# Last states of GpSimdE's quads copied by ScalarE, and half of the fifth quad to GpSimdE in every pass

## The chip, the cores and the metric

One core of a Trainium2 chip runs the whole program in one launch. The metric is the device time of an execution in microseconds. A kernel is timed in several runs and the median counts. One further execution is recorded by the hardware profiler: its trace gives the start and the length of every instruction on the engines TensorE (PE), VectorE (DVE), ScalarE (ACT), GpSimdE (POOL) and on the DMA queues, which SyncE (SP) mostly feeds.

## What is computed

The input is `x`, two images of 256 channels and 4096 positions. A state-space layer (a Mamba block with 256 inner channels) is added to it, then two more, one that runs forward over the positions and one that runs backward (512 inner channels each), then a mixture of 8 experts of three dense layers. The change touches only the recurrence of the three state-space layers, which is this, for every inner channel `d` and each of 16 states `s`:

```python
def step(h, inp):
    dt_t, B_t, C_t, x_t = inp
    h = h * exp(dt_t[..., None] * A) + (dt_t * x_t)[..., None] * B_t[:, None, :]
    y = einsum('bds,bs->bd', h, C_t)
    return (h, y)
```

So for each channel and state there is a decay `exp(dt * A)`, an input `dt * x * B`, a linear recurrence over 4096 positions, a product with `C`, and a sum over the 16 states.

## The kernel before

**Tiling.** Each layer of each image is a job (`Scan`); there are 6, with `nj` = 2, 4 and 4 blocks of 128 channels for each image. A job runs over 8 chunks of `T` = 512 positions. A chunk of a job is a step; a step has `nj / 2` passes; a pass treats two blocks of channels in 8 quads, `n` = 0 to 7. That makes 48 steps, 80 passes and 640 quads (`quads`, L665), numbered `g`. "Even" and "odd" passes below are those with `g // QN` even or odd, counted from 0. A quad is a tile of 128 rows by 4 groups of 512 positions. A row is one of 32 channels together with one of four states, so that a quad covers 128 channels and 4 of their 16 states.

**The work on a quad** comes from these small functions.
- `emit_b` (L738): GpSimdE multiplies the input by `B` into the quad's tile `bq` (L742, 128x2048). `bq` has six buffers.
- `emit_decay` (L744) and `emit_join` (L757): ScalarE makes the decays of half a quad (two groups) into a PSUM tile `da` with two `Exp` (L752). There is one `da` buffer for each half. Since one scan runs over two groups at once, the decay at the border is set so that nothing passes it, and the state of the second group is added to its first input by the small activation in `emit_join` (L763), which reads the state `h`.
- `emit_scan` (L773): VectorE scans half a quad, 128x1024 (L778). The first group's state is the scan's initial value. The result goes into `bq`, where GpSimdE is to take the product with `C`, else into `da`.
- The product with `C`: VectorE does it for half a quad in `emit_times_c` (L787, from `da` into `bq`), GpSimdE for a quad in `emit_times_c_quad` (L803, in place in `bq`; 128x2048, or 128x1024 for half a quad).
- The last state of each group is kept in `job.h` for the next chunk. ScalarE copies it from `da` in `emit_carry` (L797, two values in a row) where VectorE does the product. GpSimdE copies it from `bq` at the head of `emit_times_c_quad` (L802, four values in a row, two for half a quad) where GpSimdE does it.
- `emit_sum` (L808): TensorE sums the four states of a quad into `y` (L811); `emit_gate` (L822) is VectorE's.

**Who takes which product** is told by `on_pool` (L768): the quads 0, 2 and 5 of every pass (`POOL_C`) are GpSimdE's, and in odd passes also the first half of quad 4 (`POOL_HALF`).

**Order.** The main loop (L1105) goes over quads and halves; a half is a slot. In a slot, each engine's instructions are issued in the order of the text, and `in_order` (L158) ties every instruction to the one before it on its engine, so this is the order in which each engine runs. ScalarE has in a slot: the states of the slot before (`emit_carry`), the join and the decays of the slot after (`emit_decay`), then what the slots' plan puts there (`sl.run(slot, "act")`: activations of the projections, softplus, table loads, copies out of PSUM, the experts). VectorE has its scan, then gates and other planned work, then its product. GpSimdE has at the first half of each quad what `POOL_AT` (L66) says: `b` is an input product, three or more quads ahead, `c` a product with `C`, `h` that of the half:

```python
POOL_AT = {0: "b3", 1: "c0 b4", 2: "b5", 3: "c2 b6", 4: "b7", 5: "h4 b8", 6: "c5 b9", 7: "b10"}
```

After it follow the planned products `dt * x` (`xdt`, L598). TensorE's sums are placed by `SUMS` (L65): those of quads 2 and 3 at quad 4, that of quad 4 at quad 6, those of 5 and 6 at quad 7. TensorE runs the projections, convolutions and experts in between, in order, so a sum that waits holds up what follows. The plan of slots and expert work is made beforehand and doesn't depend on the lines that the change touches.

After the last quad a second stage computes the remaining experts and adds up (L1154 and after).

Of the kernel before, what the change touches and what calls it, by code (L numbers as in the profile page):

```python
# [50 lines left out]
T = 512  # L51
# [4 lines left out]
QN = 8  # L56
# [4 lines left out]
POOL_C = (0, 2, 5)  # L61

POOL_HALF = (4, 0)
# [73 lines left out]
def hybrid_kernel(ctx: ExitStack, tc: tile.TileContext, a: dict, out: bass.AP):  # L137
    nc = tc.nc
# [55 lines left out]
    with ExitStack() as st:  # L194
# [155 lines left out]
        steps = [(job, c) for job in jobs for c in range(NCH)]  # L350
# [318 lines left out]
        bq, da, y = {}, {}, {}  # L669
        pending, wanted = [], []  # L670

        def at(g):

            i, jp, n = quads[g]
            return i, 2 * jp + n // SG, n % SG
# [92 lines left out]
        def on_pool(g, h):  # L768

            n = quads[g][2]  # L770
            return n in POOL_C or (n, h) == POOL_HALF and g // QN % 2

        def emit_scan(g, h):  # L773
            i, j, sg = at(g)
            job, c = steps[i]
            d = da[g, h].rearrange("p q t -> p (q t)")
            b = bq[g][:, 2 * h : 2 * h + 2, :].rearrange("p q t -> p (q t)")
            nc.vector.tensor_tensor_scan(  # L778
                b if on_pool(g, h) else d, d, b,
                job.h[:, j, sg, 2 * h : 2 * h + 1] if c else 0.0, ALU.mult, ALU.add,  # L780
            )
# [10 lines left out]
        def emit_carry(g, h):  # L792

            i, j, sg = at(g)
            d, two = da.pop((g, h)), slice(2 * h, 2 * h + 2)
            if not on_pool(g, h):
                nc.scalar.copy(steps[i][0].h[:, j, sg, two], d[:, :, T - 1])  # L797

        def emit_times_c_quad(g, groups=SG):
            i, j, sg = at(g)  # L800
            b = bq[g][:, :groups, :]
            nc.gpsimd.tensor_copy(steps[i][0].h[:, j, sg, :groups], b[:, :, T - 1])  # L802
            nc.gpsimd.tensor_tensor(  # L803
                b, b,
                cks[i]["bc", 1, sg].rearrange("p (o t) -> p o t", o=1).to_broadcast([P, groups, T]), ALU.mult,
            )
# [298 lines left out]
        for g in range(nq):  # L1105
            i, jp, n = quads[g]
            for h in range(2):
# [14 lines left out]
                if slot:  # L1122
                    emit_carry(*divmod(slot - 1, 2))
# [9 lines left out]
                if not on_pool(g, h):  # L1133
                    emit_times_c(g, h)

                if h == 0:
                    for what in POOL_AT.get(n, "").split():
                        m = g - n + int(what[1:])
                        if what[0] == "c":
                            emit_times_c_quad(m)  # L1140
                        elif what[0] == "h":
                            if on_pool(m, 0):
                                emit_times_c_quad(m, SG // 2)
                        else:
                            want_b(m)
# [8 lines left out]
    with ExitStack() as st:  # L1154
# [5 lines left out]
        n, x, y, acc, wts, wb, lt, w_dram = {}, {}, {}, {}, {}, {}, {}, {}  # L1160
# [160 lines left out]
        def layer(x, l, e, tag):  # L1321
            h = mk.tile([P, KC, T], F32, tag=f"h{l}", name=f"h{l}_{tag}", bufs=2 + 2 * l)
            for m in range(KC):
                ps = psp.tile([P, T], F32, tag="ps", name=f"hp{l}_{tag}_{m}")
                for k in range(KC):
                    nc.tensor.matmul(  # L1326
                        ps, we[f"W{l + 1}", e][:, k, m * P : (m + 1) * P], x[:, k, :],
                        start=(k == 0), stop=(k == KC - 1),
                    )
                nc.scalar.activation(  # L1330
                    h[:, m, :], ps, AF.Relu,
                    bias=of[:, l, e, m : m + 1], scale=sc[:, l, e, m : m + 1],
                )
            return h
# [104 lines left out]
        for at, (b, i, e) in enumerate(pairs):  # L1439
# [5 lines left out]
            h = layer(n[b, i], 0, e, f"{i}_{e}_{b}")  # L1445
# [136 lines left out]
```

## Time and profile before

| what | value |
| --- | --- |
| median of 3 runs (lowest, highest) | 4978.65 us (4976.32, 4984.62) |
| the profiled execution, and its span | 4972.65 us, 4970.9 us |
| granted TensorE clock, mean | 0.933 |
| first and last scan (L778) start | 58.1 us, 4437.4 us |
| VectorE's scans | 1280, 2276 to 2346 ns each by form |
| VectorE's products with C | 760, of half a quad |
| GpSimdE's products with C | 240 of a quad, 40 of half a quad |
| ScalarE's decays (L752), joins (L763) | 2560 of 686 ns, 1120 of 384 ns |
| GpSimdE's `xdt` products (L598) | 160 of 1274 ns |

All of the recurrence lies between the first and the last scan; what comes later is the experts' stage. Busy time of an engine is the time in which one of its instructions is shown at work. An instruction's length is not quite what it takes of its engine, since the next may start a little before its end or after a gap; where it matters, starts are subtracted.

### The profile page before, as it was taken

The numbers are of one execution on the slowest core, as the hardware profiler recorded it, in microseconds if no ns is written. First come the engines' busy times: TensorE is split into PE (matmuls) and PEld (weight loads), VectorE is DVE, ScalarE is ACT, GpSimd is POOL, SyncE is SP. The second block draws the span as 40 slices with busy tenths as digits, with TensorE's granted clock in tenths as the row PEclk, the third lists the DMA queues.
The fourth block names the chain that finished last, engine by engine and source line by source line (L and its number), as shares of the span: only waits on it lengthen the run. The fifth ranks groups of instructions, "written<-read, shape, count | busy, mean of one in ns | idle before, by whom it ended". The sixth has DMA issues, their size and how long they took to land. (4 is left out here: it accounts for less than half of the span.)

```text
span 4970.9 us, 47346 instructions
## 1 busy us (share of the span) xinstructions
PE 4225.8 (85%) x14912; PEld 1476.1 (30%) x14912; DVE 4567.6 (92%) x3097; ACT 3613.1 (73%) x7304; POOL 4340.4 (87%) x1424
## 2 busy tenths in 40 slices
PE   5777777788776899989999899889868989999999
PEld 1222222222222233333333333333222333334444
DVE  6998999999999999999999999999999999975565
ACT  5777777777777788878788788888767888862232
POOL 6998999999999999999999999999999999960000
PEclk8778899989988999999999999999989999999999
DMA  5455454444444455446676555555534455536653
GB/s 193 158 184 171 154 171 158 158 145 155 164 157 148 173 183 177 165 174 237 241 246 222 170 173 170 189 169 190 175 121 153 165 187 176 186 131 233 226 168 127
DMA packets 335407, 875.26 MB, mean 176 GB/s; under 512 B 36314, under 2 KB 111860, under 8 KB 293172
## 3 DMA queue, kind: packets, MB, share of 16 engines
q1 hardware_dynamic: 326164, 835.39, 48.7%
q0 software_dynamic: 8992, 36.85, 2.9%
q8 instruction: 118, 1.93, 0.2%
q14 instruction: 133, 1.09, 0.1%
HBM read 673.27 MB, written 198.84 MB: 175 GB/s over the span
## 5 line engine op out<-in xcount | busy, mean ns | idle before, releaser
L742 POOL TENSOR_TENSOR bq<-rxdt,bc 128x2048 f32<-128x2048 f32 x640 | 2893.8, 4544 | 15.2 <-DMA rxdt<-xdtd 7.3
L752 ACT ACTIVATE da<-rdt,w_a 128x512 f32<-128x512 f32 x2560 | 1756.9, 686 | 70.0 <-DVE bq L778 23.6
L778 DVE TENSOR_TENSOR_SCAN da<-da,h_state,bq 128x1024 f32<-128x1024 f32 x664 | 1557.9, 2346 | 50.3 <-ACT da L752 34.7
L803 POOL TENSOR_TENSOR bq<-bq,bc 128x2048 f32<-128x2048 f32 (+1 forms) x280 | 1180.1, 4215 | 22.6
L778 DVE TENSOR_TENSOR_SCAN bq<-da,h_state,bq 128x1024 f32<-128x1024 f32 x456 | 1059.0, 2338 | 8.1 <-ACT da L752 7.9
L811 PE MATMUL y<-bq,stack 128*32 128x512 f32 x5120 | 742.2, 665 | 276.5 <-POOL bq L803 251.2
L787 DVE TENSOR_TENSOR bq<-da,bc 128x1024 f32<-128x1024 f32 x760 | 926.2, 1219 | 15.7
L992 PE MATMUL e<-eh,ew 128*128 128x512 f32 x1376 | 659.5, 613 | 43.3 <-DVE sp L594 14.4
L797 ACT COPY h_state<-da 128x2 f32<-128x2 f32 x759 | 119.0, 157 | 618.8 <-DVE bq L787 615.4
L763 ACT ACTIVATE bq<-h_state,bq,a 128x1 f32<-128x1 f32 x1120 | 430.0, 384 | 4.7 <-POOL bq L742 4.1
L811 PEld LDWEIGHTS y<-bq,stack 128*32 128x32 f32 x5120 | 140.6, 116 | 823.7 <-POOL bq L803 373.6
L458 PE MATMUL z<-nx,w_in 128*128 128x512 f32 x640 | 332.6, 650 | 59.3 <-DVE q L423 21.0
L992 PEld LDWEIGHTS e<-eh,ew 128*128 128x128 f32 x1376 | 247.7, 191 | 450.4 <-issue 240.5
L531 PE MATMUL conv<-xs,w_conv 64*64 64x512 f32 x2560 | 334.6, 603 | 22.7 <-ACT xs L515 20.4
L992 PE MATMUL e<-en,ew 128*128 128x512 f32 x688 | 324.8, 605 | 26.5 <-DVE xr L891 17.6
L458 PE MATMUL xs<-nx,w_in 128*128 128x512 f32 x640 | 318.9, 626 | 31.2 <-DVE sz L624 18.4
L1330 ACT ACTIVATE h<-hp,of,sc 128x512 f32<-128x512 f32 x168 | 130.6, 777 | 275.2 <-PE hp L1326 273.7
L843 PE MATMUL o<-sz,w_out 128*128 128x512 f32 x640 | 295.8, 601 | 0.0
L1005 ACT ACTIVATE eh<-e,of,sc 128x512 f32<-128x512 f32 x344 | 260.1, 768 | 47.3 <-PE e L992 46.9
L598 POOL TENSOR_TENSOR xdt<-sp,xc 128x512 f32<-128x512 f32 x160 | 203.2, 1274 | 43.6 <-DVE sp L594 43.6
L778 DVE TENSOR_TENSOR_SCAN da<-da,bq 128x1024 f32<-128x1024 f32 x96 | 219.4, 2285 | 2.6 <-issue 1.5
L458 PEld LDWEIGHTS z<-nx,w_in 128*128 128x128 f32 x640 | 125.1, 205 | 262.1 <-issue 147.8
(145 smaller groups left out, 4753.5 us busy)
## 6 DMA issues: line engine op xcount, KB each, us to landing
rxdt<-xdtd SPq DMA_DIRECT2D x160, 1024.0 KB, 6.0
rdt<-dtd SPq DMA_DIRECT2D x160, 1024.0 KB, 6.8
bc<-bcd SPq DMA_DIRECT2D x384, 256.0 KB, 3.2
ew<-in_W SPq DMA_DIRECT2D x172, 256.0 KB, 4.9
u<-u SPq DMA_DIRECT2D x86, 512.0 KB, 5.7
u<-eu SPq DMA_DIRECT2D x82, 512.0 KB, 4.4
dtd<-sp SPq DMA_DIRECT2D x160, 256.0 KB, 3.3
xdtd<-xdt SPq DMA_DIRECT2D x160, 256.0 KB, 3.4
```

The source lines that it names most:

```text
L458: nc.tensor.matmul(ps, job.matrices["in", half][:, k, j * P : (j + 1) * P], rhs, start=(k == 0), stop=(k == KC - 1),)
L531: nc.tensor.matmul(v[r][64 * col : 64 * col + 64, :], job.matrices["conv"][rows, 2 * jp + j, k, :], ck["xs", jp][rows, j, k : k + T] if k ...
L742: nc.gpsimd.tensor_tensor(bq[g], ck["rxdt", j], over_groups(ck["bc", 0, sg]), ALU.mult)
L752: nc.scalar.activation(da[g, h][:, k, :], cks[i]["rdt", j][:, q, :], AF.Exp, scale=steps[i][0].w["a"][:, j, q * SG + sg : q * SG + sg + 1],)
L763: nc.scalar.activation(bq[g][:, q, 0:1], job.h[:, j, sg, q : q + 1], AF.Identity, scale=cks[i]["a0", j][:, h, sg : sg + 1], bias=bq[g][:, ...
L778: nc.vector.tensor_tensor_scan(b if on_pool(g, h) else d, d, b, job.h[:, j, sg, 2 * h : 2 * h + 1] if c else 0.0, ALU.mult, ALU.add,)
L787: nc.vector.tensor_tensor(bq[g][:, two, :], d, cks[i]["bc", 1, sg].rearrange("p (o t) -> p o t", o=1).to_broadcast([P, 2, T]), ALU.mult,)
L803: nc.gpsimd.tensor_tensor(b, b, cks[i]["bc", 1, sg].rearrange("p (o t) -> p o t", o=1).to_broadcast([P, groups, T]), ALU.mult,)
L811: nc.tensor.matmul(y[i, j][q * CG : (q + 1) * CG, :], stack, bq[g][:, q, :], start=False, stop=(sg == SG - 1),)
L843: nc.tensor.matmul(v[m], job.w["out"][:, j, m * P : (m + 1) * P], ck["sz", j], start=False, stop=(j == job.nj - 1),)
L992: nc.tensor.matmul(ps, ew[l][:, k, m * P : (m + 1) * P], key[x][:, k, :], start=(k == 0), stop=(k == KC - 1),)
L1005: nc.scalar.activation(key[dst][:, m, :], key["ps", l, m], AF.Relu, bias=of[:, l, e, m : m + 1], scale=sc[:, l, e, m : m + 1],)
```

## The change

GpSimdE's copy of the last states leaves `emit_times_c_quad`. `emit_carry` makes it on ScalarE, from `bq`, once per quad, after the second half's scan: four values in a row. For the fifth quad (`n` = 4), where GpSimdE has the first half alone, ScalarE copies two values from `bq` after that half's scan, and two from `da` after the other half's, as before. `on_pool` no longer asks for an odd pass, so the first half of quad 4 is GpSimdE's in every pass: its scan writes `bq`, VectorE's product of that half goes in the even passes, and `emit_times_c_quad(m, SG // 2)` is issued there at quad 5.

```diff
         def on_pool(g, h):
 
             n = quads[g][2]
-            return n in POOL_C or (n, h) == POOL_HALF and g // QN % 2
+            return n in POOL_C or (n, h) == POOL_HALF
 
...
             d, two = da.pop((g, h)), slice(2 * h, 2 * h + 2)
             if not on_pool(g, h):
                 nc.scalar.copy(steps[i][0].h[:, j, sg, two], d[:, :, T - 1])
+            elif h or not on_pool(g, 1):
+                upto = 2 * h + 2
+                nc.scalar.copy(steps[i][0].h[:, j, sg, :upto], bq[g][:, :upto, T - 1])
 
         def emit_times_c_quad(g, groups=SG):
             i, j, sg = at(g)
             b = bq[g][:, :groups, :]
-            nc.gpsimd.tensor_copy(steps[i][0].h[:, j, sg, :groups], b[:, :, T - 1])
             nc.gpsimd.tensor_tensor(
                 b, b,
                 cks[i]["bc", 1, sg].rearrange("p (o t) -> p o t", o=1).to_broadcast([P, groups, T]), ALU.mult,
```

## The prediction

> **What bounds the kernel now.** I read the busy shares first, then the groups by line with shapes kept apart, the waits of GpSimdE, the busy time of stretches, and last the timeline of one pass.
>
> ```profile
> PE 4225.8 (85%) x14912; PEld 1476.1 (30%) x14912; DVE 4567.6 (92%) x3097; ACT 3613.1 (73%) x7304; POOL 4340.4 (87%) x1424
> DVE  6998999999999999999999999999999999975565
> POOL 6998999999999999999999999999999999960000
> ...
> L742 POOL TENSOR_TENSOR bq<-rxdt,bc 128x2048 f32<-128x2048 f32 x640 | 2893.8, 4544 | 15.2 <-DMA rxdt<-xdtd 7.3 <-issue 7.3 <-PE y L811 0.6
> L803 POOL TENSOR_TENSOR bq<-bq,bc 128x2048 f32<-128x2048 f32 x240 | 1086.1, 4525 | 19.4
> L803 POOL TENSOR_TENSOR bq<-bq,bc 128x1024 f32<-128x1024 f32 x40 | 94.0, 2349 | 3.2
> L802 POOL COPY h_state<-bq 128x4 f32<-128x4 f32 x240 | 49.8, 208 | 36.2 <-DVE bq L778 36.0
> L802 POOL COPY h_state<-bq 128x2 f32<-128x2 f32 x40 | 10.7, 268 | 0.0
> L787 DVE TENSOR_TENSOR bq<-da,bc 128x1024 f32<-128x1024 f32 x760 | 926.2, 1219 | 15.7
> L797 ACT COPY h_state<-da 128x2 f32<-128x2 f32 x759 | 119.0, 157 | 618.8 <-DVE bq L787 615.4 <-DVE kept L305 1.6
> ...
> 1525.00:2382.00 857.00, 760.25 (x2720) 267.58 (x2713) 840.92 (x530) 682.57 (x1398) 852.46 (x266) 0.96 0.52 181
> 2382.00:2711.00 329.00, 300.11 (x978) 108.69 (x977) 308.02 (x185) 267.51 (x551) 316.78 (x97) 0.96 0.70 238
> 2711.00:3365.00 654.00, 589.09 (x2155) 202.75 (x2154) 645.46 (x420) 534.09 (x1075) 648.70 (x211) 0.96 0.55 176
> 3581.00:4336.00 755.00, 642.10 (x2400) 218.02 (x2398) 742.64 (x482) 587.29 (x1207) 751.06 (x239) 0.94 0.46 163
> ...
> 1800.89 2.33 DVE L778 TENSOR_TENSOR_SCAN da<-da,h_state,bq 128x1024 f32<-128x1024 f32 x1
> 1802.15 1.28 ACT L660 ACT_TABLE_LOAD   x1
> 1803.44 0.39 ACT L763 ACTIVATE bq<-h_state,bq,a 128x1 f32<-128x1 f32 x1
> 1802.98 0.19 POOL L802 COPY h_state<-bq 128x4 f32<-128x4 f32 x1
> 1803.25 4.53 POOL L803 TENSOR_TENSOR bq<-bq,bc 128x2048 f32<-128x2048 f32 x1
> 1835.61 2.36 POOL L803 TENSOR_TENSOR bq<-bq,bc 128x1024 f32<-128x1024 f32 x1
> 1837.92 4.57 POOL L742 TENSOR_TENSOR bq<-rxdt,bc 128x2048 f32<-128x2048 f32 x1
> ```
>
> The shares hide two stages: until about 4440 us VectorE and GpSimdE are both full; then the experts' tail runs on TensorE and GpSimdE is empty. The change touches the first stage alone; I take the tail as shifted, not changed. In the stretches (busy PE, PEld, DVE, ACT, POOL after the length) GpSimdE fills 99.5% of 1525 to 2382 (passes 26 to 41) and of 3581 to 4336 (passes 64 to 77), and no wait of it is listed there: it sets the pace. Elsewhere it sometimes waits for a scan, in front of its copy of states (L802): 36.0 us in 29 places, of which 6.5 in 176 to 402, 6.4 in 402 to 526, 5.0 in 526 to 1305, 4.3 in 1305 to 1525, 9.3 in 2382 to 2711, 1.8 in 2711 to 3365, 1.9 in 3365 to 3581. There VectorE, or ScalarE behind it, sets the pace.
>
> **What the Trainium skill says.** "Perfetto Trace Analysis", Optimization Strategy: the most-contended engine can change from regime to regime, and each is read by its own gaps. The trace agrees: two regimes inside one stage. "GPSIMD Engine Reference", 3.1 Elementwise: a two-input fp32 product of 2048 takes 4497 ns there, twice VectorE's. The rows say 4525 and 4544, and 2349 for half. "SBUF — State Buffer", Who interferes with whom: a VectorE instruction with at most one SBUF input, outside the two-port modes, doesn't contend with GpSimdE. Scans and products here read da from PSUM and one SBUF tile, and the L742 durations have 4543 for median and 4504 for minimum, so I stretch nothing. "Perfetto Trace Analysis", Optimizing Scalar/DVE Operations: ScalarE's access overhead is about 93 ns on SBUF, 51 on PSUM, and a profiled latency about twice that. L797 (from PSUM) shows 157 ns and the small SBUF copies L514 and L517 183 and 197; they agree.
>
> **The change by parts**, per pair of passes (one even, one odd; 40 pairs).
> GpSimdE's copies go. From L802's start to L803's is 0.27 us (1802.98 to 1803.25), duration and gap; 7 per pair: -1.89. (Busy 60.5 and the 22.6 idle ahead of L803 give 0.297 on the mean; the excess is a dozen long copies next to a DMA issue, which I don't count as gained.)
> The half product in even passes is added: 1835.61 to 1837.92, +2.31. Sum for GpSimdE +0.42 per pair, +16.8 in all; with 0.297, +0.23 and +9.3.
> VectorE loses one L787 in each even pass. Next start after one is 1.13 us later (1821.97 to 1823.10), and a scan followed by its product takes 2.38 (1815.36 to 1817.74) where one followed by another scan takes 2.24: -1.27 per pair, -51 in all. The scan itself only changes where it writes (2346 against 2338 ns): nothing.
> ScalarE gains 7 copies per pair. No row shows this form; from below the 0.04 by which L763 follows L797 (1806.97 to 1807.01), from above the full 0.20 of L517. I take 0.10, half of it, as the skill's page has it: +0.7 per pair, 28 in all (11 to 56). Queued behind each are the join (L763) and the two decays of the next slot, which VectorE's next but one scan needs. The decays already waited for that same scan to free da, so nothing new blocks them but the copy and, behind it, the join: 0.20 + 0.39 + 1.40 from the end of the scan, against 2.24 + 1.13 until VectorE wants them (a product quad follows each of quads 0 and 2). Hidden, except where ScalarE is already late: VectorE's waits for da are 3.5 us in 402 to 526 and 14.8 in 2382 to 2711. Four pairs of 0.7: +2.8. In even passes the copy of quad 4's first half no longer stands behind an L787: a small gain, counted as nothing.
> GpSimdE's product overwrites bq, so it now waits for ScalarE's copy. Behind it stand the next products, and TensorE's sums wait for those. In pass 31 the scan ends at 1803.22, ScalarE comes out of its table load at 1803.43, the copy could be done at 1803.63; GpSimdE got there at 1802.98. Read so, pass by pass, it would be late in 60 places by 61 us in all: about 0.7 us at quad 0 of the odd passes of 26 to 41 and 64 to 77, 2.5 in those of 49 to 63. I take it as nothing, for this reason: GpSimdE's lag behind VectorE at quad 0 is now uneven (4.5 us in even, 2.0 in odd passes, as in 30 and 31), because the half is taken in odd passes alone. After the change, even passes cost GpSimdE 2.31 - 0.81 more and VectorE 1.27 less, so it comes 2.8 us later, relative to VectorE, to quad 0 of the odd pass: behind the copy, not ahead of it.
>
> **The sum by stretch.** Each gets +0.42 per pair less the waits listed, but no better than VectorE's -1.27 per pair. 1525 to 2382, 8 pairs: +3.4. 3581 to 4336, 7: +2.9. 2711 to 3365, 6: 2.5 - 1.8 = +0.7. 526 to 1305, 7: 2.9 - 5.0 = -2.1. 3365 to 3581, 2: 0.8 - 1.9 = -1.1. At the floor: 176 to 402, 2: -2.5; 402 to 526, 1: -1.3; 1305 to 1525, 2: -2.5; 2382 to 2711, 3: -3.8. The first and last pair: 0. Together -6.3, with ScalarE's 2.8: -3.5. The profiled execution took 4972.65 (span 4970.9), so 4969; the three runs have their median 6.0 higher, at 4978.65, and there the same change makes 4975.
>
> **Rivals.**
> A, a wash (this sum): 4975, own range 4964 to 4986.
> B, VectorE's relief arrives. For: VectorE is at 98% too, and in 526 to 1305 and 2711 to 3581 the two share the pace; GpSimdE's gaps there include 0.08 us ahead of each L803, and dense lag may keep it from ever waiting. Against: 99.5% in 30 passes can't shrink. If the 24 pairs outside these 15 (less the last) get 1.27 each, -30, plus 6.3, and no ScalarE cost: 4955. With the mean copy (0.297) a little more.
> C, slower: GpSimdE waits for ScalarE's copy. Place: quad 0 of odd passes, behind the table load. It decides if the lag there stays under 2.7 us, because TensorE, held by GpSimdE's sums, holds ScalarE and so VectorE as well. Price 0.7 x 15 + 2.5 x 7 = 28 on 6.3, less the 13 gained at the floors and in 526 to 1305: +21, 5000.
> D, ScalarE is the bound: all 28 us on the path, with the +6.3 and nothing gained: 5013. Against: ScalarE is 80% busy where GpSimdE rules, and waits 615 us at L797.
>
> **How the numbers follow.** A measurement of this kernel tells 0.2% (10 us) from no change. Chances: A 0.45, B 0.32, C 0.19, D 0.04. A splits 0.11 faster, 0.32 same, 0.02 slower; B 0.28 and 0.04 same; C 0.02 same, 0.17 slower; D slower. So faster 0.39, same 0.38, slower 0.23. The range reaches from B with the full gain to C: 4948 to 5002; A alone 4964 to 4986.
>
> **What would show it.** Right: L802 gone, 80 half products, 720 L787, about 1040 copies of ScalarE; GpSimdE's busy time near 4374 (4340 + 94 - 60) and idle under 40 until 4430; VectorE's waits longer in passes 26 to 41. C shows as GpSimdE waiting for ScalarE's copy at L803, over 10 us in sum. B shows as stretches of 526 to 1305 and 2711 to 3581 shorter by over 1 us per pair. Wrong in any case if passes 26 to 41 get shorter: then GpSimdE did not set the pace there.

## The result, and the profile after

The changed kernel takes 5011.09 us (median of 4 runs, 5006.35 to 5015.03), beside 4977.62 for the kernel before (4 runs, 4976.32 to 4984.62). The ratio is 1.0065, with a 95% interval of 1.0053 to 1.0077: slower, by some 33 us, where 4975 had been forecast. The profiled execution took 5006.35 us, its span is 5004.6, and the mean granted clock is 0.93 (0.933 before), so the clock explains nothing.

First the busy shares and the tenths of VectorE and GpSimdE, of the changed kernel:

```profile
PE 4216.6 (84%) x14912; PEld 1471.6 (29%) x14912; DVE 4539.7 (91%) x3057; ACT 3642.1 (73%) x7584; POOL 4381.3 (88%) x1184
DVE  6998999999999999999999999999999999974565
POOL 6898999999999999999999999999999999961000
```

At this grain only single tenths differ, two of GpSimdE's and one of VectorE's. The groups by line, shapes kept apart, show that the work moved as the diff says:

```profile
L742 POOL TENSOR_TENSOR bq<-rxdt,bc 128x2048 f32<-128x2048 f32 x640 | 2983.9, 4786 | 13.3 <-DMA rxdt<-xdtd 7.3 <-PE y L813 5.9
L805 POOL TENSOR_TENSOR bq<-bq,bc 128x2048 f32<-128x2048 f32 x240 | 1143.9, 4766 | 46.2 <-ACT h_state L800 42.5 <-PE gm L337 1.6 <-POOL bq L742 1.3
L787 DVE TENSOR_TENSOR bq<-da,bc 128x1024 f32<-128x1024 f32 x720 | 877.6, 1219 | 14.5
L805 POOL TENSOR_TENSOR bq<-bq,bc 128x1024 f32<-128x1024 f32 x80 | 208.7, 2609 | 12.9 <-ACT h_state L800 12.9
```

L805 is the product with C in place (L803 before), L800 ScalarE's new copy. There are 80 half products and 720 of VectorE's, and no copy is left on GpSimdE. Two things stand out. L805 now waits for ScalarE's copy. And GpSimdE's products seem to have become longer, 4786 ns where 4544 stood before; this is a matter of how a length is recorded. From one start to the next a full product takes 4.49 us on the mean in both kernels. The long records, of over 4.8 us, nearly all lie in passes 8 to 23 and 44 to 63, and the median spacing behind them is 4.49 us too. The Trainium skill says so as well ("Perfetto Trace Analysis", GPSIMD Engine Instruction: time them by the spacing of starts). All lengths of GpSimdE's work below are spacings of starts.

The waits of the changed kernel (total, times, longest one):

```profile
ACT h_state L797 <- DVE bq L787: 529.1, 436, 23.5
...
DVE da L778 <- ACT da L752: 70.5, 80, 4.5
...
POOL bq L805 <- ACT h_state L800: 55.3, 32, 11.8
```

Before, GpSimdE waited 36.0 us for VectorE's scans in front of its copy; now 55.3 for ScalarE in front of its product. VectorE's waits for decays have doubled from 35.7. One wait of ScalarE alone has 23.5 us.

A total doesn't tell which of these count. For that I cut both traces at the first scan of passes, the same points of the work in each, and compare the lengths (us; worked out from the starts of the scans):

```
passes            before   after   longer   as forecast
0-1                118.0   133.9    +15.9        0.0
2-7                349.7   351.4     +1.7       -3.1
8-21               779.1   778.3     -0.8       -2.1
22-25              220.3   217.3     -3.0       -2.5
26-41              856.8   867.4    +10.6       +3.4
42-47              328.6   325.9     -2.7       -1.7
48-59              654.6   654.5     -0.1       +0.7
60-63              215.3   220.1     +4.8       -1.1
64-77              755.2   763.8     +8.6       +2.9
78-79              104.1   104.2     +0.1        0.0
before, behind     589.2   587.8     -1.4        0.0
```

So the loss lies in two kinds of places: 15.9 us in the first pair of passes, where nothing had been forecast, and 24.0 in passes 26 to 41 and 60 to 77, where 5.2 had been. Passes 2 to 7 lie 4.8 us above the forecast; the rest is within 1.4 us of it.

**The first pair.** The timeline of VectorE, GpSimdE and ScalarE in pass 1 of the changed kernel (start, length, engine, and in brackets the idle time ahead and what ended it):

```profile
130.59 0.67 DVE L594 SCALAR_TENSOR_TENSOR sp<-dt,sp 128x512 f32<-128x512 f32 x1
131.18 22.08 DVE L920 TENSOR_TENSOR sc<-sc,bn 128x32 f32<-128x32 f32 x1
153.18 0.18 DVE L921 TENSOR_TENSOR of<-bn 128x32 f32<-128x32 f32 x1
...
128.38 9.03 POOL L742 TENSOR_TENSOR bq<-rxdt,bc 128x2048 f32<-128x2048 f32 x2
137.36 2.49 POOL L598 TENSOR_TENSOR xdt<-sp,xc 128x512 f32<-128x512 f32 x2
139.80 4.50 POOL L805 TENSOR_TENSOR bq<-bq,bc 128x2048 f32<-128x2048 f32 x1
144.25 8.95 POOL L742 TENSOR_TENSOR bq<-rxdt,bc 128x2048 f32<-128x2048 f32 x2
165.03 2.35 POOL L805 TENSOR_TENSOR bq<-bq,bc 128x1024 f32<-128x1024 f32 x1 [11.82 <-ACT h_state L800]
...
158.56 0.16 ACT L797 COPY h_state<-da 128x2 f32<-128x2 f32 x1 [23.45 <-DVE bq L787]
```

And the same place in the kernel before (L918 to L921 there are L920 to L923 after):

```profile
131.90 0.26 DVE L918 TENSOR_TENSOR sc<-sc,bn 128x32 f32<-128x32 f32 x1
132.08 4.56 DVE L919 TENSOR_TENSOR of<-bn 128x32 f32<-128x32 f32 x1
136.68 1.19 DVE L920 TENSOR_TENSOR of<-of,sc 128x32 f32<-128x32 f32 x1
137.90 1.19 DVE L921 TENSOR_TENSOR of<-of,bn 128x32 f32<-128x32 f32 x1
...
127.57 9.03 POOL L742 TENSOR_TENSOR bq<-rxdt,bc 128x2048 f32<-128x2048 f32 x2
136.55 2.49 POOL L598 TENSOR_TENSOR xdt<-sp,xc 128x512 f32<-128x512 f32 x2
138.98 0.19 POOL L802 COPY h_state<-bq 128x4 f32<-128x4 f32 x1
```

`shift()` (inside `scales`) is four small operations of VectorE on 128x32, once in the whole program. Each of them reads two operands in SBUF (the second one two parts of the same tile), as GpSimdE's products do. In the kernel before, the second of them already took 4.56 us, until GpSimdE went from its second product to `xdt` at 136.55, and the last two 1.19 each, one `xdt` product each. After the change the first takes 22.08 us: through seven instructions of GpSimdE, back to back, until the last ends, at 153.2, and GpSimdE has nothing to start. It has nothing because VectorE stands: no scan, so no copy of the state (11.82 us of waiting), and ScalarE stands for 23.45. The four operations now take VectorE from 131.18 to 153.73, 22.6 us, where they took from 131.90 to 139.01, 7.1. The difference, 15.4, is nearly all of the 15.9 that this pair loses.

**Passes 26 to 77.** Pass 31 of the changed kernel, the same moment as in the timeline that the prediction shows:

```profile
1807.13 1.92 PE L813 MATMUL y<-bq,stack 128*32 128x512 f32 x16 [2.25 <-POOL bq L805]
1815.44 3.60 PE L845 MATMUL o<-sz,w_out 128*128 128x512 f32 x8
...
1819.07 0.59 ACT L860 COPY xr<-o 128x512 f32<-128x512 f32 x1 [2.23 <-PE o L845]
1819.67 1.28 ACT L660 ACT_TABLE_LOAD   x1
1820.97 0.20 ACT L800 COPY h_state<-bq 128x4 f32<-128x4 f32 x1
1821.07 0.38 ACT L763 ACTIVATE bq<-h_state,bq,a 128x1 f32<-128x1 f32 x1
1821.24 4.53 POOL L805 TENSOR_TENSOR bq<-bq,bc 128x2048 f32<-128x2048 f32 x1 [0.70 <-ACT h_state L800]
...
1822.79 2.36 DVE L778 TENSOR_TENSOR_SCAN da<-da,h_state,bq 128x1024 f32<-128x1024 f32 x1 [0.87 <-ACT da L752]
```

This is case C of the prediction. The scan that made the state was over at 1816.29, but on ScalarE a copy out of PSUM comes first, which waits 2.23 us for TensorE, then a table load; only then the copy of the state. TensorE in turn had waited 2.25 us for GpSimdE's product of the pass before, until 1807.13, and from there it had no gap up to the product L845 that ScalarE's copy waits for: what GpSimdE waits for hangs on its own earlier work. GpSimdE loses 0.70 us, and behind the same pile VectorE's next scan is 0.87 late for its decays. The busy time in these stretches (length; busy PE, PEld, DVE, ACT, POOL) agrees:

```profile
1538.74:2406.12 867.38, 761.73 (x2722) 265.81 (x2715) 832.30 (x523) 688.43 (x1454) 862.35 (x218) 0.95 0.51 179
3606.59:4370.39 763.80, 641.25 (x2397) 215.83 (x2396) 735.48 (x476) 593.29 (x1255) 759.64 (x198) 0.94 0.46 161
```

GpSimdE is idle for 5.03 us of the first and 4.16 of the second, all ahead of L805. The rest is more work: from GpSimdE's first instruction of pass 26 to its first of pass 42, waits taken off, a pair of passes takes it 107.18 us where it took 106.64 (+0.54), and in passes 64 to 77 108.42 where it took 107.85 (+0.57). In passes 60 to 63 it is 108.86 for 107.96 (+0.90), and its waits there grew from 1.93 to 3.94 us. The forecast had +0.42.

### The profile page after: what moved, and what is told of

Read it like the earlier page. It is cut to its first block, busy times and chain, and to the rows that moved or that the text cites. A ratio compares the mean times of both kernels' runs of the same rounds, so it can differ in the third digit from the quotient of the medians.

```text
span 5004.6 us, 47517 instructions
## 1 busy us (share of the span) xinstructions
PE 4216.6 (84%) x14912; PEld 1471.6 (29%) x14912; DVE 4539.7 (91%) x3057; ACT 3642.1 (73%) x7584; POOL 4381.3 (88%) x1184
## 3 DMA queue, kind: packets, MB, share of 16 engines
q8 instruction: 118, 1.93, 0.2%
## 5 line engine op out<-in xcount | busy, mean ns | idle before, releaser
L742 POOL TENSOR_TENSOR bq<-rxdt,bc 128x2048 f32<-128x2048 f32 x640 | 2983.9, 4786 | 13.3 <-DMA rxdt<-xdtd 7.3
L778 DVE TENSOR_TENSOR_SCAN da<-da,h_state,bq 128x1024 f32<-128x1024 f32 x630 | 1478.5, 2347 | 83.4 <-ACT da L752 67.5
L805 POOL TENSOR_TENSOR bq<-bq,bc 128x2048 f32<-128x2048 f32 (+1 forms) x320 | 1352.6, 4227 | 59.0 <-ACT h_state L800 55.3
L778 DVE TENSOR_TENSOR_SCAN bq<-da,h_state,bq 128x1024 f32<-128x1024 f32 x490 | 1139.1, 2339 | 13.6 <-ACT da L752 13.6
L787 DVE TENSOR_TENSOR bq<-da,bc 128x1024 f32<-128x1024 f32 x720 | 877.6, 1219 | 14.5
L797 ACT COPY h_state<-da 128x2 f32<-128x2 f32 x719 | 112.5, 157 | 532.7 <-DVE bq L787 529.1
L458 PE MATMUL z<-nx,w_in 128*128 128x512 f32 x640 | 320.1, 629 | 63.8 <-ACT nx L493 24.7
L845 PE MATMUL o<-sz,w_out 128*128 128x512 f32 x640 | 298.9, 606 | 0.0
L598 POOL TENSOR_TENSOR xdt<-sp,xc 128x512 f32<-128x512 f32 x160 | 231.6, 1462 | 40.7 <-DVE sp L594 40.7
L778 DVE TENSOR_TENSOR_SCAN da<-da,bq 128x1024 f32<-128x1024 f32 x90 | 205.7, 2285 | 5.1 <-ACT da L752 3.0
```

What stands on the lines that cost most here:

```text
L458: nc.tensor.matmul(ps, job.matrices["in", half][:, k, j * P : (j + 1) * P], rhs, start=(k == 0), stop=(k == KC - 1),)
L742: nc.gpsimd.tensor_tensor(bq[g], ck["rxdt", j], over_groups(ck["bc", 0, sg]), ALU.mult)
L778: nc.vector.tensor_tensor_scan(b if on_pool(g, h) else d, d, b, job.h[:, j, sg, 2 * h : 2 * h + 1] if c else 0.0, ALU.mult, ALU.add,)
L787: nc.vector.tensor_tensor(bq[g][:, two, :], d, cks[i]["bc", 1, sg].rearrange("p (o t) -> p o t", o=1).to_broadcast([P, 2, T]), ALU.mult,)
L805: nc.gpsimd.tensor_tensor(b, b, cks[i]["bc", 1, sg].rearrange("p (o t) -> p o t", o=1).to_broadcast([P, groups, T]), ALU.mult,)
L845: nc.tensor.matmul(v[m], job.w["out"][:, j, m * P : (m + 1) * P], ck["sz", j], start=False, stop=(j == job.nj - 1),)
```

## The experiments

The expectations name their theories by letters. W: GpSimdE's product waits for ScalarE's copy behind the table load. L: no wait matters, GpSimdE just has more to do. S: the stall of VectorE at `shift()` is a loss by itself, apart from the other two. Other letters are spelt out where they stand. Ratios are against runs of the kernel before made together with each set; its medians there were 4978.31 us in the first set (E1 to E4), 4977.46 in the second (P1, P2, H1, H2) and 4977.13 in the third (E5, E6).

### E1: the copies alone

ScalarE copies, but the half product stays in odd passes. Against the changed kernel:

```diff
-            return n in POOL_C or (n, h) == POOL_HALF
+            return n in POOL_C or (n, h) == POOL_HALF and g // QN % 2
```

> Only the first part of the change: ScalarE copies the states, GpSimdE has the half of quad 4 in odd passes alone, as before. Theory W (GpSimdE's product waits for ScalarE's copy, and ScalarE is held by TensorE, which GpSimdE's sums hold): the copies save GpSimdE 1.9 us per pair, of which the waits at quad 0 of the odd passes take back 0.7 to 2.5; with the one long stall of VectorE in pass 1 (about 16 us) the time is within 10 us of before, 4970 to 4990. Theory L (only GpSimdE's load counts): 15 pairs at -1.9, VectorE then setting the pace: 4955 to 4965, and 16 more if the stall stays. Theory H (the added half is harmless, the copies alone cost): as slow as the changed kernel, 5005 to 5015.

Measured: 4995.41 us, ratio 1.0031 (1.002 to 1.0042). GpSimdE has less work than in the kernel before, and the program is slower than that one. L is out, at least alone; H, by which the copies alone cost as much as the whole change, is out as well; and the total is 5 us above what W had. First, VectorE's stall is here too, and the first pair is 12.7 us longer than before, most of the 17 that this kernel loses:

```profile
130.96 19.76 DVE L920 TENSOR_TENSOR sc<-sc,bn 128x32 f32<-128x32 f32 x1
```

Second, in passes 26 to 41 GpSimdE's work per pair falls from 106.64 to 104.90 us, 13.9 in eight pairs, and the stretch is as long as before (857.8 against 856.8). GpSimdE's waits in that stretch, in one row:

```profile
POOL bq L805 <- ACT h_state L800: 15.6, 8, 4.0
```

15.6 us, once in each odd pass: the whole saving is spent in front of ScalarE's copy. So W's wait takes any time that GpSimdE saves, unless the lag grows.

### E2: the half product alone

The kernel before, with the half product in every pass and the copies left on GpSimdE:

```diff
-            return n in POOL_C or (n, h) == POOL_HALF and g // QN % 2
+            return n in POOL_C or (n, h) == POOL_HALF
```

> Only the second part: GpSimdE keeps its copies and takes the half of quad 4 in every pass. Theory L: +2.6 us per pair where GpSimdE sets the pace (15 pairs, +39) and +1 to +2 in the 14 pairs where the pace is shared: 5025 to 5045. Theory W says the same here, since no copy of ScalarE is waited for, and no stall of 16 us in pass 1, because the gap between copy and product is still there. Theory H: about 4980.

Measured: 5052.96 us, ratio 1.014 (1.0125 to 1.0156), above the range expected. GpSimdE waits for nothing in passes 26 to 41 and takes 109.19 us per pair, +2.55; the prediction's prices make 2.31 + 0.27 = 2.58 for this edit. In passes 64 to 77 it is +2.58. So GpSimdE does set the pace there, the price of the half product was right, and of the two edits this is the costly one. Passes 8 to 21 and 48 to 59 lost 13.1 and 10.0 us, 1.8 per pair, as the expectation had it for a shared pace. What goes beyond its range is spread: passes 26 to 41 and 64 to 77 lost 44.2 us where it had 39, passes 60 to 63 lost 6.6, and some 9 came in the first and last pair and outside of the recurrence. The mean granted clock of this run was 0.922; what of these 9 goes to that stays open. At `shift()` there was no long stall:

```profile
131.16 2.92 DVE L918 TENSOR_TENSOR sc<-sc,bn 128x32 f32<-128x32 f32 x1
134.00 4.54 DVE L919 TENSOR_TENSOR of<-bn 128x32 f32<-128x32 f32 x1
```

VectorE got in where GpSimdE went from one product to the next, at about 134.0, and again at its next change, at 138.5. No copy ran at either of them, so the gap behind a copy, by which the expectation explains it, isn't directly what let VectorE in. The stall thus belongs to the copies' move, not to the half product.

### E3: `shift()` on GpSimdE

The changed kernel, with the four small operations issued on GpSimdE, at the same slot:

```diff
-                nc.vector.tensor_tensor(sc, sc, bn[:, :, M_G], ALU.mult)
+                nc.gpsimd.tensor_tensor(sc, sc, bn[:, :, M_G], ALU.mult)
...
-            sl.put(s0 - 11, "dve", shift)
+            sl.put(s0 - 11, "pool", shift)
```

(The other three operations likewise.)

> The changed kernel with the four small operations of L920 to L923 on GpSimdE's queue instead of VectorE's. Theory S (a VectorE instruction with two SBUF inputs gets no turn while GpSimdE's reading instructions follow one another without a gap; L920 took 22.1 us in the changed kernel): pass 1 is shorter by about 16 us, the whole 4992 to 4998. If L920's length is a mark of something else that stops VectorE there, no change: 5005 to 5015.

Measured: 4992.85 us, ratio 1.0027 (1.0016 to 1.0037). The first pair goes from 133.9 to 110.2 us; L920 takes 0.255 us on GpSimdE. That is 23.7 us less than in the changed kernel, and 7.8 less than in the kernel before, which paid for its own stall. The stretches of passes 26 to 41 and 60 to 77 stay within 1.1 us of the changed kernel's. The whole gains 18 by the medians, less than the pair alone: in the profiled execution passes 42 to 47 are 3.6 us longer than after and what lies outside the recurrence 8.4; the latter differs by as much between the executions profiled here. So S is shown, as a cause of its own.

### E4: the state's copy first

The changed kernel, with ScalarE's copy for GpSimdE's quads moved up: right after the scan that it reads, ahead of what the plan puts on ScalarE in that slot (the copy out of PSUM and the table load among it). For slots of these quads:

```diff
-                if slot:
+                if slot and not on_pool(*divmod(slot - 1, 2)):
                     emit_carry(*divmod(slot - 1, 2))
                 emit_decay(*divmod(slot + 1, 2))
-                sl.run(slot, "act")
+                if not on_pool(g, h):
+                    sl.run(slot, "act")
...
                 emit_scan(g, h)
+                if on_pool(g, h):
+                    emit_carry(g, h)
+                    sl.run(slot, "act")
```

> The changed kernel, with ScalarE's copy of a GpSimdE quad put ahead of the planned ScalarE work of its slot, so that it no longer stands behind a copy out of PSUM that waits for TensorE, nor behind a table load. Theory W: GpSimdE's waits for the copy (55.3 us in 32 places, 11.8 of it in pass 1) fall under 20, passes 26 to 41 and 64 to 77 lose 0.7 us per pair: 4995 to 5003. Theory L: the waits were cover for other lateness, and the time stays at 5005 to 5015. Against both: planned ScalarE work comes up to 1 us later in every GpSimdE slot; if that decides, slower than 5015.

Measured: 5009.42 us, ratio 1.0059 (1.0047 to 1.0072): the total missed its range. By stretch it did what W says: passes 26 to 41 are 5.4 us shorter than after, 60 to 63 5.0, 64 to 77 5.0, and GpSimdE's waits there have all but gone. But now every planned work of ScalarE in such a slot waits for a scan, in all passes. VectorE, which waits for that work:

```profile
DVE xc L544 <- ACT thx L540: 60.4, 53, 11.9
```

In the changed kernel this wait came to 35.2 us in 20 places. Passes 22 to 25 lost 6.3, 2 to 7 3.5, and 7 came from the end of the program, which varies by so much between executions. The fix was too broad, so E5 narrows it.

### E5: the copy first at quad 0 of odd passes only

As E4, where `slot % 16 == 1` in an odd pass (the second half of quad 0), and nowhere else. The copy's old place in the next slot is left out there.

```diff
-                if slot:
-                    emit_carry(*divmod(slot - 1, 2))
+                if slot % 16 != 2 or g // QN % 2 == 0:
+                    if slot:
+                        emit_carry(*divmod(slot - 1, 2))
                 emit_decay(*divmod(slot + 1, 2))
-                sl.run(slot, "act")
+                first = slot % 16 == 1 and g // QN % 2
+                if not first:
+                    sl.run(slot, "act")
...
                 emit_scan(g, h)
+                if first:
+                    emit_carry(g, h)
+                    sl.run(slot, "act")
```

> The changed kernel, with ScalarE's copy put ahead of its planned work at one place only: quad 0 of the odd passes, where the earlier trial lost nothing and won 5.4 us in passes 26 to 41, 5.0 in 60 to 63 and 5.0 in 64 to 77. Theory W: these gains without the losses of the earlier trial, 13 to 16 us: 4995 to 4999. If the gain there was bought by the other 240 places, no change: 5008 to 5014.

Measured: 4997.53 us, ratio 1.0035 (1.0023 to 1.0046), as expected. Passes 26 to 41 are 5.0 us shorter than after, 60 to 63 2.9, 64 to 77 4.9. Pass 31 again:

```profile
1817.68 0.18 ACT L800 COPY h_state<-bq 128x4 f32<-128x4 f32 x1
1819.97 0.59 ACT L860 COPY xr<-o 128x512 f32<-128x512 f32 x1 [2.11 <-PE o L845]
1820.58 1.28 ACT L660 ACT_TABLE_LOAD   x1
...
1821.27 4.67 POOL L805 TENSOR_TENSOR bq<-bq,bc 128x2048 f32<-128x2048 f32 x1
```

The copy is done at 1817.86, GpSimdE comes to its product 3.4 us later and doesn't wait. ScalarE's wait for TensorE and its table load are where they were; they just stand behind the copy now. In passes 26 to 41 GpSimdE's time per pair is 107.36 with its waits, where the changed kernel has 107.81: what remains over 106.64 is the load (0.50) and 0.22 of waits.

### E6: both repairs

E5 with E3's `shift()` on GpSimdE.

> The same, with L920 to L923 on GpSimdE's queue. If the two causes are apart and are all there is: 5011 less 14 less 18: 4976 to 4983, the time before. If there is a third one: over 4985.

Measured: 4971.47 us, ratio 0.9989 (0.9982 to 0.9995), below the range expected: this had 18 us for `shift()`, and the first pair alone gives 24.0. With the two causes repaired the time is that of the kernel before. But this kernel is also rid of the stall that the kernel before has of its own; beside that kernel without its stall (H1 below, 4968.31) it is 3.2 us longer. GpSimdE's larger load is still there: against the kernel before, passes 26 to 41 are 6.5 us longer, 60 to 63 2.2 and 64 to 77 3.4.

### P1 and P2: what a small operation of VectorE waits for

The stall came with the copies' move, though no copy runs during it. To see whether it happens elsewhere, both kernels got `shift()` on GpSimdE and 12 probes on VectorE, on tiles that nothing else uses, in passes 12, 33, 54 and 70: two products that read two SBUF tiles, and between them one that reads one. P1 is the changed kernel, P2 the kernel before.

```diff
+            nc.vector.tensor_tensor(probe[:, :32], probe[:, 32:64], probe[:, 64:], ALU.mult)
...
+            nc.vector.tensor_scalar(probe[:, :32], probe[:, 32:64], 1.0, None, ALU.mult)
...
+        for p in (12, 33, 54, 70):
+            sl.put(16 * p + 2, "dve", two_inputs)
+            sl.put(16 * p + 6, "dve", one_input)
+            sl.put(16 * p + 9, "dve", two_inputs)
```

> The changed kernel with L920 to L923 on GpSimdE, and twelve probes on VectorE's queue, three each in passes 12, 33, 54 and 70: two products of 128x32 with both inputs in SBUF, and between them a tensor_scalar of the same size with one input. They compute nothing that is used. Theory S: the two-input probes take from 4 to over 20 us, until GpSimdE runs dry, the one-input probes 0.2. If a two-input probe gets in at the next boundary of GpSimdE's instructions, as L919 did before, none takes over 4.6, and the 22 us of pass 1 were an accident of that place.

> The kernel before, with the same four small operations on GpSimdE and the same twelve probes. Theory S in its form with the gap (the copy of GpSimdE and the 0.08 us behind it let VectorE in): no two-input probe takes more than about 9 us, the way from one copy of GpSimdE to the next. If the copies are not what lets VectorE in, the probes are as long here as in the changed kernel.

Each was run once, for its trace; the times, 5046.5 and 4992.76 us, include the probes. The probe's rows (least, median and greatest length in ns) in P1:

```profile
L1053 DVE TENSOR_TENSOR probe<-probe x8: 181/1846/15054, 745.4 to 3997.6; 128x32 f32<-128x32 f32 x8
L1056 DVE TENSOR_SCALAR probe<-probe x4: 172/1535/3161, 771.0 to 3984.1; 128x32 f32<-128x32 f32 x4
```

and in P2:

```profile
L1051 DVE TENSOR_TENSOR probe<-probe x8: 224/2043/4218, 744.7 to 3956.8; 128x32 f32<-128x32 f32 x8
L1054 DVE TENSOR_SCALAR probe<-probe x4: 896/2151/3924, 757.7 to 3943.3; 128x32 f32<-128x32 f32 x4
```

In P1 three of the eight products with two inputs take 12.8, 15.1 and 14.4 us, past two or three changes of GpSimdE's instruction, until GpSimdE has run dry. In P2 none passes even one: all eight end with the instruction of GpSimdE that runs, 4.2 us at most. Four of them get in at a change from one product to the next with no copy there, and so do four of P1's eight. `shift()` itself was long in all four kernels that left it on VectorE and have no copies on GpSimdE (22.08, 19.76, and 22.64 and 21.61 in E4 and E5), and short in both that have them. The one-input probe had been meant as a control at 0.2 us, and that was wrong: it takes up to 3.9 us, until GpSimdE's instruction ends, though never longer. (The rule that the prediction quotes exempts an instruction with one SBUF input only outside the two-port modes; the runs don't show in which mode this one ran.)

So wherever such an operation of VectorE met a running instruction of GpSimdE here, it waited for its end, and in kernels without the copies in GpSimdE's stream it could lose several in a row. Eight probes a kernel are few; the six kernels with `shift()` on VectorE point the same way. Why a change of instruction lets VectorE in with the copies and not always without them stays open: the gaps between instructions look alike, several got in where no copy was, and in the kernel before the last copy had been made at 122.8, long before VectorE got in at 136.6.

### H1: the kernel before with `shift()` on GpSimdE

E3's edit on the kernel before.

> The kernel before with L918 to L921 on GpSimdE's queue. They took 7.2 us of VectorE in pass 1 (0.3, 4.6, 1.2, 1.2). Theory S: about 7 us less, 4968 to 4974. If GpSimdE sets the pace in pass 1, nothing: 4976 to 4980.

Measured: 4968.31 us, ratio 0.9984 (0.9976 to 0.9992). The first pair takes 109.8 us instead of 118.0: the kernel before had this fault too, at 8.2 us.

### H2: the half where VectorE sets the pace

E3, with the half product in even passes only where the changed kernel had been shorter than E1.

```diff
-            return n in POOL_C or (n, h) == POOL_HALF
+            p = g // QN
+            return n in POOL_C or (n, h) == POOL_HALF and (p % 2 or 8 <= p < 26 or 42 <= p < 48)
```

> ScalarE copies everywhere, the four small operations on GpSimdE, and the half of quad 4 in every pass only in passes 8 to 25 and 42 to 47, where the changed kernel was shorter than the one with the copies alone (778.3 against 781.5, 217.3 against 220.4, 325.9 against 329.8 us); in odd passes elsewhere. If the stretches add up: 4995 less 20 in pass 1 less 10: 4962 to 4968, less than before and than the changed kernel. If the stretches depend on one another, or the copies alone lose elsewhere: 4970 to 4980.

Measured: 4968.76 us, ratio 0.9983 (0.9976 to 0.999): just above the first range of the expectation and below the second. Faster than both kernels of this study, but not told apart from H1, which is the kernel before and one small edit.

## Why the prediction was wrong

**The first pair: 0 forecast, +15.9 measured.** The step that failed is "so I stretch nothing", and with it "The first and last pair: 0". The page was the right one: "SBUF — State Buffer", Who interferes with whom, also says that a VectorE instruction with two SBUF inputs contends with a GpSimdE instruction that reads SBUF. The check behind the step looked at scans and VectorE's products alone, because they make up VectorE's time, and not at the four operations of `shift()`, of which the trace before has one at 4.56 us for a form that takes 0.26 beside it. No case of the prediction had this mechanism. Its size could hardly have been read from before, where no such operation lost a second time. E3 gives it: 23.7 us against none, of which the kernel before paid 7.8.

**"I take it as nothing": the wait for ScalarE's copy.** The reasoning was that GpSimdE would come 2.8 us later to quad 0 of the odd passes, behind the copy. GpSimdE did come later: in pass 31 it was 2.0 us behind the scan that made the state before the change, and 4.3 after it. The step left out what the text of case C says itself: TensorE, held by GpSimdE's sums, holds ScalarE. Where GpSimdE sets the pace, ScalarE's work slips with it: the end of its table load moved from 2.5 to 4.7 us behind the same scan. So the lag against ScalarE didn't grow. GpSimdE came 0.65 us before the copy could be done, by the prediction's reading, and in fact waited 0.70. (That reading takes 1803.22 for the end of the scan in question. This is the scan after it; the state's own scan ended at 1800.97. Nothing hangs on it, since the table load ended later than both.) C's price for passes 26 to 41 and 64 to 77, 0.7 x 15 = 10.5, stands against 5.03 + 4.16 = 9.2 of measured waits. In passes 60 to 63 it waits 3.9 us, 2.0 more than before, of the 4.8 lost. Only in 49 to 59 did C charge too much: these passes did not get longer. E1 shows the other side: with the half taken away, the lag shrinks and the wait becomes 1.95 us per odd pass. So C was the right mechanism for these passes, at a chance of 0.19, and it gave 5000; with the stall that would be 5016. That it lies 5 us from what was measured is in part luck: C's sum charges seven odd passes in 49 to 63 where there are eight, takes off 13 where its own figures make 12.2, and those passes lost little.

**GpSimdE's load: +0.42 per pair was mis-sized.** It measured +0.54 and +0.57. E2 has the half product right (2.55 and 2.58 with its copy, 2.58 forecast); E1 has the copies' going at 1.74 instead of 1.89, so that a copy saved 0.25 us and not 0.27. Over 15 pairs the difference to the forecast is 2 us.

**What held.** GpSimdE sets the pace in passes 26 to 41 and 64 to 77: its 4381.3 us of busy time stand against the 4374 forecast, and E2 shows that a microsecond given to it there is lost. The relief at the floors came in passes 22 to 25 (-3.0, forecast -2.5) and 42 to 47 (-2.7, -1.7), but in 2 to 7 it did not (+1.7, -3.1). B was wrong: passes 8 to 21 and 48 to 59 gained 0.9 us together. D was wrong, though its 5013 is by chance the nearest of the four: E6 has all of ScalarE's copies, and it loses 3.2 us to H1, not 34. ScalarE's copy costs what was taken: 188 ns shown, 0.10 us from its start to the next (1820.97 to 1821.07). The page's rule, from which half the shown length was taken, fits less well for the copy out of PSUM than the prediction says: twice 51 ns is 102, and L797 shows 157.

**The sum.** Stall 15.9; added waits in passes 26 to 41 and 60 to 77 5.03 + 4.16 + 2.01 = 11.2; load there, 8 x 0.54 + 7 x 0.57 + 2 x 0.90 = 10.1: 37.2 of the 39.9 that the table has in these places. The rest, 2.7, lies in where the cuts fall, since the table cuts at VectorE's scans and the load is counted between GpSimdE's starts. The other stretches gave 6.2 back, and so the span grew by 33.7. With stall and most of the waits repaired the change comes to the wash of case A: E6 takes 4971.47 us, H1, without the change but with the same `shift()`, 4968.31. So the change gains nothing even then.

## What to carry to other kernels

Where an engine takes over a small step in front of an in-place operation, look at what stands ahead of that step in the new engine's order at the moment that counts, and ask whether the engine that one relies on to be late isn't itself what makes the other late. Before declaring engines independent, look through the trace for single instructions that are ten times longer than others of their form, not only at the groups that fill the time: one of them, run once, was nearly half of this loss. And a saving on the engine that sets the pace is worth something only if its next wait doesn't lie within the saving, as E1 shows.

## What was unexpected in the hardware

A VectorE product of 128x32 with two SBUF inputs, 0.18 us when GpSimdE is idle, took 22.08 us beside seven back-to-back instructions of GpSimdE and ended only with the last of them. I had expected a wait for one instruction at most. Three probes and four executions of this product, between 12.8 and 22.6 us, show that it can lose several times in a row. A `tensor_scalar` of the same size with one SBUF input waited too, up to 3.9 us, but never past the instruction that was running. With short copies in GpSimdE's stream no operation waited past a change of instruction: 0 of 8 probes, where 3 of 8 did without them, and none of `shift()`'s in two kernels, where its first did in four of four. The cause of this difference is not known.
